# Turning the rows of the ternary weight by DMA instead of by TensorE, in a gated attention and feed-forward kernel

## The chip, the cores and the metric

The kernel runs on one core of a Trainium2 chip. The core has TensorE (PE, matrix products), VectorE (DVE), ScalarE (ACT), GpSimd (POOL) and SyncE (SP). SP and POOL mainly issue DMAs here, and the DMAs of all queues are carried by the core's 16 DMA engines. The metric is the device time of one execution in microseconds (us), the median of several.

## The reference

There are two batches of 1024 rows; a row has 2048 numbers. W is a 2048 x 2048 weight.

```python
def fake_quant(x, scale, zp):
    q = clip(round(x / scale + zp), 0, 255)
    return (q - zp) * scale

h   = x + tanh(g_xattn) * fake_quant(layernorm(x)) @ fake_quant(ctx)      # per batch: 1024x2048 @ 2048x2048

y   = layernorm(h)
s   = 127 / max(|y|) of each row
yq  = clip(round(y * s), -128, 127) / s
sw  = 1 / mean(|W|)
tw  = clip(round(W * sw), -1, 1)                                          # -1, 0 or 1
out = h + tanh(g_ffn) * (yq @ tw.T) / sw
```

The second product needs W's input index on the partitions (the axis that TensorE sums over), while W lies in memory with its output index first. So each block of 128 rows of W is rounded to bytes, limited to -1, 0 and 1, and turned.

## The kernel before

The function `centred` (line 344) runs when the zero points are 128. Rows are handled in tiles of 128, so a batch has 8 tiles (`MT`); `resid` holds the 8 tiles of the batch in work and is reused by the second one. An `arena` of 32 slots in SBUF holds everything large: loaded f32 rows (two slots each, `wide`), the quantized context (one slot for 256 of its rows and half of its columns), the turned activations (`aT` for the first product, `qT` for the second), and the turned W (`wt`, 8 slots, each with four row blocks and half of the input index, in float8). A pool named q8 (`bytes_`, `NB` = 4 buffers of 128x2048 bytes) holds a tile between its rounding and its turning. PSUM gives three accumulators `mm` and two small buffers `tr` for turning.

Bytes are turned as pairs: two neighbouring bytes are seen as one 16-bit value, TensorE transposes 128x128 of these against an identity matrix into `tr` (lines 494 and 1035), and the result holds pairs (j = 0, 1) side by side, which the later matmuls read with a stride. For the activations, two copies of 128x1024 from `tr` make f16 (line 502). For W, `weight_turn` (line 1021) does, for each of the 16 row blocks `ot`: `quant` on ACT (line 1028: f32 to rounded bytes, in a q8 buffer), `turn` on PE (eight transposes, line 1035), and `clip` twice (two halves of 1024 columns, from `tr` to float8 in a slot of the arena), on DVE as a max and min (line 1045) or on ACT as a sign (line 1043).

The work runs in these stages, which overlap: the first product of batch 0 (`first`, matmuls of line 622, in two halves h of the columns, evicted by DVE at line 628); loading W once for its mean (`weight_load`, line 977, `weight_sum`); `norm2`, which gives `qT` (lines 660, 666, 716); turning W, for which nine of the 16 blocks are loaded a second time; the second product of batch 0, in pairs of tiles with one quarter q of the output columns (`couple`, matmuls of line 759, q = 0 in single row blocks of W) and then tile by tile (`plain`, line 805), evicted by DVE at line 743 and stored by SP (line 750); meanwhile loads of batch 1's context (line 589) and rows (line 468) on POOL's queue; sums and differences of W's quarters on DVE (line 842), written to DRAM and brought back; then batch 1: first product (line 622) and the second one in seven products instead of eight (`seven`, line 930).

The order on each engine is fixed when the kernel is built. Every piece is a `step` of the planner `Order` (line 108), with an engine (or a choice of two, of which the planner takes the one that ends first), an estimated duration, a due time, what it reads and writes, the buffer that it takes and those that it gives back, and for DMAs the time that they hold the DMA engines. The planner lays all steps out twelve times, moves due times back from the end each time, and keeps the shortest layout. Each engine then works through its list in that order, and a step whose input is late holds up all those behind it on its engine.

Of the kernel before, what the change touches and what calls it, by code (L numbers as in the profile page):

```python
# [11 lines left out]
I16 = mybir.dt.int16  # L12
F8 = mybir.dt.float8e4
AF = mybir.ActivationFunctionType
ALU = mybir.AluOpType
# [8 lines left out]
class Plan:  # L24
# [9 lines left out]
    def step(self, engine, weight, due, do, rd=(), wr=(), take=None, give=(), dma=0.0, hold=0.0):  # L34
        n = len(self.steps)
        after = set()
        for key in rd:
            if key in self.writer:
                after.add(self.writer[key])
        for key in wr:  # L40
            after.update(self.readers.pop(key, ()))
            if key in self.writer:
                after.add(self.writer[key])
            self.writer[key] = n
        for key in rd:
            self.readers.setdefault(key, []).append(n)
        after.discard(n)
        self.steps.append((engine, weight, due, do, after, take, tuple(give), dma, hold))
        return n
# [58 lines left out]
class Order:  # L108
# [64 lines left out]
    def run(self, due):  # L173
        steps, N = self.steps, len(self.steps)
        waits = [len(s[3]) for s in steps]
        early = [s[7] for s in steps]
        pools = {k: [(0.0, -1)] * n for k, n in self.sizes.items()}
        left = dict(self.users)
        till = {}
        free, open_ = {}, {}  # L180
        dma_free, dma_last = 0.0, -1
        begin, end, where, slots = [0.0] * N, [0.0] * N, [None] * N, [None] * N
        pred = [[] for _ in steps]
        links = self.links = [{} for _ in steps]
        last = {}
        order = []

        def put(n):
            for e, w in steps[n][0]:
                open_.setdefault(e, {})[n] = w  # L190

        for n in range(N):
            if not waits[n]:
                put(n)
        for _ in range(N):
            best = None
            for e, cand in open_.items():
                fe = free.get(e, self.START.get(e, self.BRANCH))
                for n, w in cand.items():
                    at = early[n]  # L200
                    if at < fe:
                        at = fe
                    if best is not None and at > best[0] + 1e-6:
                        continue
                    take = steps[n][4]
                    if take:
                        at = max(at, self.room(pools[take[0]], *take[1:]))
                        if at == float("inf"):
                            continue
                    if len(steps[n][0]) > 1:  # L210
                        key = (at, due[n], n, at + w, e)
                    else:
                        key = (at, due[n], n, 0.0, e)
                    if best is None or at < best[0] - 1e-6 or key[1:] < best[1:]:
                        best = key
            if best is None:
                self.stuck = [n for c in open_.values() for n in c], order, slots
                return None
            at, _, n, _, e = best
            ways, _, _, _, take, give, dma, _ = steps[n]  # L220
            if len(ways) > 1:
                ends = []
                for e2, w2 in ways:
                    ends.append((max(at, free.get(e2, self.BRANCH)) + w2, e2, w2))
                fin, e, w = min(ends)
                at = fin - w
            else:
                w = ways[0][1]
            for e2, _ in ways:
                del open_[e2][n]  # L230
            if take:
                pool = pools[take[0]]
                idx = slots[n] = self.pick(pool, at, *take[1:])
                for i in idx:
                    if pool[i][1] >= 0:
                        pred[n].append(pool[i][1])
                        links[n][pool[i][1]] = True
                    pool[i] = (float("inf"), -1)
            if e in last:
                pred[n].append(last[e])  # L240
            last[e] = n
            begin[n] = at
            where[n] = e
            fin = at + w
            free[e] = fin
            if dma:
                if dma_last >= 0:
                    pred[n].append(~dma_last)
                dma_free = max(dma_free, fin) + abs(dma)
                dma_last = n  # L250
                fin = dma_free + self.LANDING
            end[n] = fin
            order.append(n)
            for m, i in give:
                for j in range(steps[m][4][1]) if i is None else (i,):
                    left[m, j] -= 1
                    t = till.get((m, j))
                    if t is None or fin + self.LAG > t[0]:
                        t = (fin + self.LAG, n)
                    till[m, j] = t  # L260
                    if not left[m, j]:
                        pools[steps[m][4][0]][slots[m][j]] = t
            for m in self.follow[n]:
                same = len(steps[m][0]) == 1 and steps[m][0][0][0] == e and not dma
                t = fin + (0.0 if same else self.LAG)
                if t > early[m]:
                    early[m] = t
                waits[m] -= 1
                if not waits[m]:
                    put(m)  # L270
        return order, begin, end, where, slots, pred
# [72 lines left out]
def centred(  # L344
# [15 lines left out]
    nc = tc.nc  # L360
# [5 lines left out]
    MT, OT = M // P, O // P  # L366
# [1 line left out]
    H, U = 1024, 512  # L368
    NQ = N // U
    I8 = mybir.dt.int8  # L370
    NS, NB = 32, 4
    SLOT = 2048

    const = ctx.enter_context(tc.tile_pool(name="const", bufs=1))
# [28 lines left out]
    def slot16(s):  # L403
        return arena[:, s * SLOT : (s + 1) * SLOT]
# [30 lines left out]

    Q_COST = {"PRE": 0.5, "SP": 0.5, "POOL": 0.7}
    turned = {}

    def parameters():
        s = {}  # L440
# [32 lines left out]
    def rsqrt(v, sd):  # L473
# [7 lines left out]
        nc.vector.scalar_tensor_tensor(r, e, 1.5, r0, ALU.add, ALU.mult)  # L481
        return r

    def turn_steps(t, key, q, q_by, due, name, pieces=1):

        s = {}

        def turn(i, slots=None):
            if slots is not None:
                s["pt"] = tr[slots[0]]  # L490
            pt = s["pt"].bitcast(F16).rearrange("p (c r) -> p c r", c=C)
            v = q["q"].bitcast(F16)
            for c in range(i * C // pieces, (i + 1) * C // pieces):
                nc.tensor.transpose(pt[:, c, :], v[:, ts(c, P)], ident)  # L494

        def spread(h, engine, slots=None):
            if h == 0:
                turned[name, t] = slots[0]
            d = slot16(turned[name, t]).rearrange("p (c j m) -> p c j m", c=C, j=2)
            v = s["pt"].bitcast(I8).rearrange("p (c m j) -> p c j m", c=C, j=2)  # L500
            n = C // 2
            (nc.scalar.copy if engine == "ACT" else nc.vector.tensor_copy)(  # L502
                d[:, ts(h, n)], v[:, ts(h, n)]
            )

        by = None
        for i in range(pieces):
            n = step(
                "PE", 0.05 + 0.55 / pieces, due - 50, (lambda i: lambda slots=None: turn(i, slots))(i),
                rd=[key("q", i)], wr=[key("pt", i)], take=None if i else ("tr", 1),  # L510
                give=[q_by] if i == pieces - 1 else [],
            )
            by = by if i else n
        ways = (("ACT", 1.1), ("DVE", 1.3))
        first_ = step(
            ways, 0, due - 20, lambda e, slots: spread(0, e, slots), rd=[key("pt", 0)], wr=[(name, t, 0)],
            take=("ar", 1, 0, home_t), give=[by],
        )
        step(
            ways, 0, due - 20, lambda e: spread(1, e), rd=[key("pt", pieces - 1), (name, t, 0)],  # L520
            wr=[(name, t, 1)], give=[by],
        )
        turned[name, t, "by"] = first_
# [357 lines left out]
    def seven(ta, tb, due, final=False):  # L881
# [22 lines left out]
        qa, qb = ([("qT", t, i) for i in range(2)] for t in (ta, tb))  # L904
        by = step("DVE", 0.7, due - 3, lambda slots: sums(0, slots), rd=qb, wr=[("S", ta, 1)], take=("ar", 2, 0, pairs_d))
        step("DVE", 0.7, due - 3, lambda: sums(1), rd=qa[:1], wr=qb[:1] + [("S", ta, 3)])
        step("DVE", 0.7, due - 3, lambda: sums(2), rd=qa[:1] + [("S", ta, 1)], wr=[("S", ta, 2)])
        step("DVE", 0.7, due - 3, lambda: sums(3), rd=qa[1:] + [("S", ta, 2)], wr=[("S", ta, 4)])
        products = (
            ("P1", "A", lambda: half(ta, 0), (0, 0), qa[:1], True, (ta, 0)),  # L910
            ("P2", "C", lambda: half(ta, 1), (0, 1), qa[1:], True, (ta, 0)),
# [109 lines left out]
    def weight_turn(ot, due):  # L1021
# [15 lines left out]
        def clip(h, engine, slots=None):  # L1037
# [10 lines left out]
            "ACT", 2.1, due, quant, rd=[("wl", ot), ("sw",)], wr=[key("q")], take=("q8", 1),  # L1048
            give=[wl[ot]["by"]],
        )  # L1050
        p = step("PE", 0.6, due - 50, turn, rd=[key("q")], wr=[key("pt")], take=("tr", 1), give=[by])
        for h in range(2):
            need = [key("pt")] + ([("w", q, 0, h)] if o else [])
# [946 lines left out]
```

## Time and profile before

| | |
|---|---|
| time, median of 3 runs | 492.32 us (491.85 to 495.02) |
| time of the profiled execution | 494.64 us |
| its span | 492.9 us |
| PE busy | 457.8 us, 93% of the span |
| DVE busy | 335.1 us, 68% |
| ACT busy | 262.8 us, 53% |
| transposes of W on PE, line 1035 | 128 instructions, 9.6 us busy |
| limiting of W on DVE, line 1045 | 23 instructions, 27.3 us |
| limiting of W on ACT, line 1043 | 9 instructions, 9.1 us |
| rounding of W on ACT, line 1028 | 16 instructions, 31.3 us |
| moved by DMA | 102.20 MB, mean 207 GB/s |

The span runs from the first to the last instruction that the profiler recorded; the time of an execution includes a little around it (1.74 us here). Busy time of matmuls overlaps at their ends, since they are pipelined: eight transposes in a row show 0.61 us of busy time, though the next matmul starts 0.45 us after the first of them. "PEld" is the loading of weights into TensorE, beside the matmuls.

### The profile page before, as it was taken

Reading aid. Unit: us, or ns where it says so; the run is one execution under the profiler, and the core shown is the slowest. Engines: PE = TensorE matmul, PEld = TensorE weight load, DVE = VectorE, ACT = ScalarE, POOL = GpSimd, SP = SyncE. Lnnn points to the kernel's source line nnn. Section 1 sums busy time; section 2 is a strip of 40 time slices with the busy share of each in tenths; the row PEclk is TensorE's granted clock in tenths of the full one; section 3 lists DMA queues with packets and bytes.
Section 4 is the critical chain, followed back from the end, with each engine's and each line's share of the span. In section 5 each row is a group of like instructions: output and inputs, shape, how many; then the busy total and the mean of one; then the engine's idle time right before and its main releaser. Section 6 shows DMA issues by size and latency. Waiting matters only on the chain.

```text
span 492.9 us, 6309 instructions
## 1 busy us (share of the span) xinstructions
PE 457.8 (93%) x2564; PEld 225.6 (46%) x2564; DVE 335.1 (68%) x522; ACT 262.8 (53%) x203; POOL 21.7 (4%) x39
## 2 busy tenths in 40 slices
PE   0489999999999898999998989999999999999995
PEld 0134444445576654444444435444444444444442
DVE  4778973588599897769997877223578887343432
ACT  3678987687799988831117678101366853000000
POOL 0000000000002120021011100000000000000000
PEclk9999999999999999999999999999999999999999
DMA  6999988990445985399999750053000012231304
GB/s 208 397 423 421 421 319 332 420 429 41 172 172 231 367 302 211 91 343 391 422 345 325 257 215 1 1 179 163 1 0 1 1 43 88 85 128 44 128 8 169
DMA packets 21853, 102.20 MB, mean 207 GB/s; under 512 B 1976, under 2 KB 1976, under 8 KB 16696
## 3 DMA queue, kind: packets, MB, share of 16 engines
q1 hardware_dynamic: 15008, 67.11, 34.2%
q0 software_dynamic: 6800, 34.61, 19.6%
q8 instruction: 22, 0.36, 0.3%
q14 instruction: 15, 0.12, 0.1%
q10 hardware_dynamic: 8, 0.00, 0.0%
HBM read 80.74 MB, written 20.97 MB: 206 GB/s over the span
## 4 chain that ended last, share of the span: by engine, by line
PE 65%; DMA 14%; issue 12%; DVE 3%; ACT 3%; SPq 1%; POOL 1%; POOLq 0%; ACTq 0%
PE mm L622 41%; PE mm L930 20%; DMA arena<-in_ctx_dram 14%; PE tr L494 2%; ACT arena L593 1%; ACT bytes L567 1%; PE mm L805 1%; SPq L1961 1%; DVE strip L666 1%; POOL arena L589 1%; DVE arena L1045 1%; DVE arena L502 0%; DVE resid L743 0%; PE mm L759 0%; POOL arena L977 0%
## 5 line engine op out<-in xcount | busy, mean ns | idle before, releaser
L622 PE MATMUL mm<-arena 128*128 128x512 f16 x1024 | 229.8, 383 | 7.9 <-DVE arena L597 4.6
L622 PEld LDWEIGHTS <-arena 128*128 128x128 f16 x1024 | 99.6, 99 | 125.0 <-issue 9.3
L743 DVE SCALAR_TENSOR_TENSOR resid<-mm,am,resid 128x1024 f32<-128x1024 f32 (+1 forms) x53 | 58.1, 1097 | 59.7 <-PE mm L930 47.9
L930 PE MATMUL mm<-arena 128*128 128x512 fp8e4 x448 | 97.5, 379 | 0.0
L593 ACT ACTIVATE arena<-arena,scal 128x2048 int16<-128x2048 f32 x32 | 63.3, 1999 | 47.3 <-DMA arena<-in_ctx_dram 36.4
L628 DVE SCALAR_TENSOR_TENSOR resid<-mm,scal,resid 128x1024 f32<-128x1024 f32 x32 | 40.9, 1278 | 49.4 <-PE mm L622 38.1
L930 PEld LDWEIGHTS <-arena 128*128 128x128 f16 x448 | 43.7, 98 | 51.9
L759 PE MATMUL mm<-arena 128*128 128x128 fp8e4 (+1 forms) x448 | 58.5, 288 | 1.7 <-DVE resid L743 1.7
L805 PE MATMUL mm<-arena 128*128 128x512 fp8e4 x256 | 55.9, 379 | 0.0
L660 ACT ACTIVATE arena<-resid,strip 128x2048 f32<-128x2048 f32 x16 | 32.0, 1998 | 39.5 <-DVE strip L654 35.4
L502 ACT CAST arena<-tr 128x1024 f16<-128x1024 int8 x39 | 37.8, 1011 | 16.9 <-PE tr L494 7.5
L759 PEld LDWEIGHTS <-arena 128*128 128x128 f16 x448 | 33.4, 98 | 24.1 <-issue 2.0
L666 DVE TENSOR_REDUCE strip<-arena 128x1 f32<-128x2048 f32 x16 | 36.5, 2280 | 5.1 <-ACT arena L660 5.1
L531 DVE BATCH_NORM_STATS2 stats<-resid 128x6 f32<-128x512 f32 x64 | 39.7, 675 | 0.0
L805 PEld LDWEIGHTS <-arena 128*128 128x128 f16 x256 | 24.9, 98 | 29.5
L567 ACT ACTIVATE bytes<-resid,strip 128x2048 int8<-128x2048 f32 (+1 forms) x17 | 33.0, 1987 | 7.7 <-DVE strip L550 5.9
L716 ACT ACTIVATE bytes<-resid,strip 128x2048 int8<-128x2048 f32 x16 | 32.7, 2087 | 6.7 <-DVE strip L689 6.7
L842 DVE TENSOR_TENSOR arena<-arena 128x2048 fp8e4<-128x2048 fp8e4 x16 | 36.0, 2281 | 0.0
L502 DVE CAST arena<-tr 128x1024 f16<-128x1024 int8 x25 | 30.3, 1218 | 7.1 <-PE tr L494 6.8
L1028 ACT ACTIVATE bytes<-arena,scal 128x2048 int8<-128x2048 f32 x16 | 31.3, 1999 | 0.8 <-DVE scal L1014 0.8
L1045 DVE TENSOR_SCALAR arena<-tr 128x1024 fp8e4<-128x1024 int8 x23 | 27.3, 1216 | 6.1 <-PE tr L1035 6.1
L494 PE MATMUL tr<-ident,bytes 128*128 128x128 f16 x256 | 20.6, 225 | 11.5 <-ACT bytes L567 9.2
(59 smaller groups left out, 184.5 us busy)
## 6 DMA issues: line engine op xcount, KB each, us to landing
arena<-in_ctx_dram SPq DMA_DIRECT2D x16, 1024.0 KB, 15.4
arena<-in_L_ffn_weight_dram SPq DMA_DIRECT2D x16, 1024.0 KB, 12.6
arena<-in_ctx_dram POOLq DMA_DIRECT2D x16, 1024.0 KB, 8.7
out_dram<-resid SPq DMA_DIRECT2D x31, 512.0 KB, 4.7
arena<-in_L_ffn_weight_dram POOLq DMA_DIRECT2D x9, 1024.0 KB, 6.6
resid<-in_x_dram POOLq DMA_DIRECT2D x8, 1024.0 KB, 11.6
resid<-in_x_dram SPq DMA_DIRECT2D x7, 1024.0 KB, 14.7
awayT<-arena SPq DMA_DIRECT2D x8, 512.0 KB, 7.5
```

What stands on the lines that cost most here:

```text
L502: (nc.scalar.copy if engine == "ACT" else nc.vector.tensor_copy)(d[:, ts(h, n)], v[:, ts(h, n)])
L531: nc.vector.bn_stats(stats6[:, t % 4, c, :], res(t)[:, ts(c, 512)])
L567: nc.scalar.activation(q["q"][:, ts(g, w)], res(t)[:, ts(g, w)], AF.Identity, bias=s["bi"][:, i : i + 1], scale=s["sc"][:, i : i + 1],)
L593: nc.scalar.activation(slot16(slots[0]).bitcast(I16), s["w"], AF.Identity, scale=rs2)
L622: nc.tensor.matmul(pm[t][:, ts(q, U)], a[:, c, j, :], o[:, j, ts(q, U)], start=(c + j == 0), stop=(c + j == C),)
L628: nc.vector.scalar_tensor_tensor(v, pm[t], g1, v, ALU.mult, ALU.add, accum_out=acc[:, i : i + 1])
L666: nc.vector.tensor_reduce(s["vm"][:, n + i : n + i + 1], s["dev", t], AX.X, ALU.max)
L743: lambda: nc.vector.scalar_tensor_tensor(v, ps(), am2[:, t : t + 1], v, ALU.mult, ALU.add),
L759: nc.tensor.matmul(ps[:, o0 * P : o1 * P], a[:, c, j, :], w[:, j, o0:o1], start=(c + j == 0), stop=(c + j == C),)
L805: nc.tensor.matmul(s["pm"][:, ts(i, U)], a[:, c, j, :], w[:, j, :], start=(c + j == 0), stop=(c + j == C),)
L842: nc.vector.tensor_tensor(slot8(s[k, n])[:, w], slot8(at(a))[:, w], slot8(at(b))[:, w], op, saturate=False)
L930: nc.tensor.matmul(s[bank][:, ts(n, U)], a[:, c, j, :], v[:, c, j], start=new and c + j == 0, stop=c + j == 4, skip_group_check=not new,)
```

## The change

W's row blocks no longer go through TensorE and PSUM. After the rounding on ACT, a DVE instruction (`flat`) limits all 2048 bytes of each row in place in the q8 buffer, reading int8 and writing float8. Two DMAs on SP's queue then turn the block, each for half of it: the source is 128 rows of 512 pairs of bytes, seen as int16, and the destination is the place in the arena's slot where `clip` wrote before. The q8 buffer is given back by the two DMAs instead of by the transposes on PE, and there are five such buffers instead of four. The planner counts a turning DMA with its own time to landing. `turn_far` would do the same for activations, but `by_dma` names only blocks of W, so it is never called. In `seven`, two sums also count as readers that give back a slot of `qT`.

```diff
-                fin = dma_free + self.LANDING
+                fin = dma_free + self.LANDING if dma > 0 else fin - 2 * dma + self.LANDING
...
-    NS, NB = 32, 4
+    NS, NB = 32, 5
...
+    by_dma = {("w", ot) for ot in range(OT)}
...
     def turn_steps(t, key, q, q_by, due, name, pieces=1):
 
+        if (name, t) in by_dma:
+            return turn_far(t, key, q, q_by, due, name)
...
-        step("DVE", 0.7, due - 3, lambda: sums(2), rd=qa[:1] + [("S", ta, 1)], wr=[("S", ta, 2)])
-        step("DVE", 0.7, due - 3, lambda: sums(3), rd=qa[1:] + [("S", ta, 2)], wr=[("S", ta, 4)])
+        step("DVE", 0.7, due - 3, lambda: sums(2), rd=qa[:1] + [("S", ta, 1)], wr=[("S", ta, 2)], give=[turned["qT", ta, "by"]])
+        step("DVE", 0.7, due - 3, lambda: sums(3), rd=qa[1:] + [("S", ta, 2)], wr=[("S", ta, 4)], give=[turned["qT", ta, "by"]])
...
             "ACT", 2.1, due, quant, rd=[("wl", ot), ("sw",)], wr=[key("q")], take=("q8", 1),
             give=[wl[ot]["by"]],
         )
+        if ("w", ot) in by_dma:
+
+            def flat():
+                nc.vector.tensor_scalar(s["q"].bitcast(F8), s["q"], -1.0, 1.0, ALU.max, ALU.min, saturate=False)
+
+            def far_turn(h, slots=None):
+                if slots is not None:
+                    wt[q, h] = slots[0]
+                d = slot16(wt[q, h]).bitcast(I16)[:, ts(o, U)].rearrange("p (c m) -> p c m", c=4)
+                nc.sync.dma_start_transpose(d, s["q"].bitcast(I16)[:, ts(h, U)])
+
+            step("DVE", 1.3, due, flat, wr=[key("q")])
+            for h in range(2):
+                step(
+                    "SP", 0.8, due, (lambda h: lambda slots=None: far_turn(h, slots))(h),
+                    rd=[key("q")] + ([("w", q, 0, h)] if o else []), wr=[("w", q, o, h)],
+                    take=None if o else ("ar", 1, 0, home_w), give=[by], dma=-0.8,
+                )
+            return
         p = step("PE", 0.6, due - 50, turn, rd=[key("q")], wr=[key("pt")], take=("tr", 1), give=[by])
```

More of the change, by code (lines that the diff above doesn't have):

```diff
@@ L482, in rsqrt, with turn_far, turn, spread @@
         return r
+    def turn_far(t, key, q, q_by, due, name):
+        def turn(slots):
+            turned[name, t] = slots[0]
+            d = slot16(slots[0]).bitcast(I16)[:, H:].rearrange("p (c r) -> p c r", c=C)
+            nc.sync.dma_start_transpose(d, q["q"].bitcast(I16))
+        def spread(h, engine):
+            d = slot16(turned[name, t]).rearrange("p (c j m) -> p c j m", c=C, j=2)
+            v = slot16(turned[name, t])[:, H:].bitcast(I8).rearrange("p (c m j) -> p c j m", c=C, j=2)
+            n = C // 2
+            (nc.scalar.copy if engine == "ACT" else nc.vector.tensor_copy)(d[:, ts(h, n)], v[:, ts(h, n)])
+        n = turned[name, t, "by"] = step(
+            "SP", 1.1, due, turn, rd=[key("q", 0)], wr=[(name, t, 0), (name, t, 1)], take=("ar", 1, 0, home_t),
+            give=[q_by], dma=-1.4,
+        )
+        step((("ACT", 1.1), ("DVE", 0.75)), 0, due, lambda e: spread(0, e), wr=[(name, t, 0)])
+        step("ACT", 1.1, due, lambda: spread(1, "ACT"), rd=[(name, t, 0)], wr=[(name, t, 1)])
     def turn_steps(t, key, q, q_by, due, name, pieces=1):
+        if (name, t) in by_dma:
+            return turn_far(t, key, q, q_by, due, name)
         s = {}
@@ L1050, in weight_turn @@
         )
+        if ("w", ot) in by_dma:
[12 more added lines that the diff above has]
+                    take=None if o else ("ar", 1, 0, home_w), give=[by], dma=-0.8,
+                )
+            return
         p = step("PE", 0.6, due - 50, turn, rd=[key("q")], wr=[key("pt")], take=("tr", 1), give=[by])
```

## The prediction

> **What bounds the kernel now.** I read the strip of the page first: PE is at nine tenths or more almost everywhere from the third slice on. Then the stage that the change touches, from the first rounding of W (123.9 us) to the limiting of its last block (202), as one window (busy us of PE, weight loads, DVE, ACT, POOL, each with its instructions; then granted clock, DMA share, GB/s):
>
> ```profile
> PE   0489999999999898999998989999999999999995
> ...
> 124.00:202.00 78.00, 73.76 (x659) 46.31 (x658) 65.75 (x101) 71.49 (x51) 10.03 (x16) 1.00 0.66 243
> ```
>
> In these 78 us PE is busy for 73.8, ACT for 71.5 and DVE for 65.8: three engines are nearly full, and DMA has a third of its time free. What W's turning costs there is in the groups by line:
>
> ```profile
> L1045 DVE TENSOR_SCALAR arena<-tr 128x1024 fp8e4<-128x1024 int8 x23 | 27.3, 1216 | 6.1 <-PE tr L1035 6.1
> L1035 PE MATMUL tr<-ident,bytes 128*128 128x128 f16 x128 | 9.6, 219 | 1.5 <-DVE arena L502 1.5
> L1043 ACT ACTIVATE arena<-tr 128x1024 fp8e4<-128x1024 int8 x9 | 9.1, 1020 | 5.7 <-DVE arena L1045 4.5 <-PE tr L1035 1.2
> ```
>
> The timeline of PE shows what a block costs TensorE, and how late W comes (start, duration, instructions, idle time before in brackets):
>
> ```profile
> 194.35 0.61 PE L494 MATMUL tr<-ident,bytes 128*128 128x128 f16 x8
> 196.49 0.61 PE L1035 MATMUL tr<-ident,bytes 128*128 128x128 f16 x8 [1.52 <-DVE arena L502]
> 196.93 3.62 PE L759 MATMUL mm<-arena 128*128 128x512 fp8e4 x16
> 200.38 0.61 PE L1035 MATMUL tr<-ident,bytes 128*128 128x128 f16 x8
> 201.39 17.43 PE L759 MATMUL mm<-arena 128*128 128x512 fp8e4 x80 [0.39 <-DVE resid L743]
> ```
>
> From the transposes' start at 196.49 to the next matmul is 0.44 us; the chain that ended last gives a block 0.45. The last block is turned only 1 us before the products of the last quarter run on, so W is made just in time. Last, that chain leaves PE between 138 and 265 us and goes through DVE, POOL's queue and the loads of batch 1:
>
> ```profile
> 229.11 19.04 DMA arena<-in_ctx_dram
> ...
> 250.54 8.72 DMA arena<-in_ctx_dram
> ...
> 262.80 2.10 ACT bytes L567
> ...
> 264.94 0.62 PE tr L494 x8
> ```
>
> So PE sets the time, and batch 1's inputs are close behind: PE waits 1.24 us at 264.9 and 2.00 at 287.9, then runs without a gap to the last eviction.
>
> **The change, part by part.**
>
> *PE loses the transposes:* 16 blocks x 0.45 us = **-7.2 us**, all on the path.
>
> *PE's waits in this stage* are 0.50 + 0.48 + 1.34 + 1.52 + 0.39 = 4.2 us. The 0.48 (a transpose waiting for line 1043) and the 1.52 (for a buffer `tr` behind DVE's copies) come from the two `tr` buffers, which W no longer takes. **-2.0**; the others wait for evictions and I leave them.
>
> *DVE and ACT:* 23 x 1.216 = 28.0 us leave DVE and 9 x 1.02 = 9.2 leave ACT. DVE gets 16 `flat` of 128x2048, int8 to float8, both in SBUF. No row has this. The bounds are line 597 (one input, 16 bits, SBUF to SBUF, same size) with 0.684 us, and line 842 (float8, two inputs, same size) with 2.281. With two inputs, 16 bits take 0.686 us for 1024 columns (line 900) and 8 bits 2.281 for 2048, so 8 bits go at half the rate. Some 0.15 us of each is fixed (line 531: 0.675 for 512, line 666: 2.280 for 2048, so 1.045 ns per column and 0.14 left). Line 597 halved in rate is 0.15 + 2 x 0.534 = **1.22 us**, the value I take, as the operation and places are those of line 597. 16 x 1.22 = 19.5: DVE -8.5, ACT -9.2. With 2.281 it would be 36.5: DVE +8.5, ACT -9.2, so nothing for the two together. These gains are not on PE's path themselves; they let W arrive earlier, which PE needs once it is faster.
>
> The Trainium skill, "VectorE: DVE Perf Modes", section "The perf-mode tier table (the rule you actually need)", gives a fp32 scalar operation in SBUF twice the plain rate, 1227 ns for 2048, and has no column for bytes. By it a `flat` would be an estimated 1.23 us; the trace of before can't show it.
>
> *The turning DMAs:* 32 on SP's queue, 128 KB each, no transposing DMA in the trace. The issue costs SP 0.33 us by the stores, and SP issues nothing between about 100 and 175.8 us; behind it stand the stores of line 750, which let batch 1's rows in. Time to landing: 4.2 us for a store of 256 KB, 4.4 for 512 KB at the start, 15.4 in the median for 1024 KB in a crowd. How long a turning DMA holds up the next one is bounded by 128 KB at the 423 GB/s of the busiest slices, 0.31 us, and by a full landing of 4.2 us. I take 1 us held and 4 us to landing: 128 KB lies nearer to the first bound by its size, but a turned block is moved in finer pieces than a plain one, so I leave it three times the plain 0.31. That fills 32 us of the queue within 75, with room.
>
> The Trainium skill pulls both ways. "VectorE: DVE Perf Modes", section "The three transpose paths", puts a 128x128 transpose at 390 ns on TensorE and 1309 ns by DMA and advises TensorE where PSUM will do. If those followed one another, 128 tiles would take an estimated 168 us and W would be some 90 us late. "DMA: Bandwidth & Descriptors", section "Latency and other measured facts", has 261 GB/s for transposing DMAs: 4.19 MB in an estimated 16 us, no bound at all. The row against the first rule is that PE's eight transposes cost 0.45 us here, not 3.1; nothing in the trace decides for the DMA.
>
> *The way of a block gets longer:* after rounding it was 0.6 (PE) + 1.2 (limiting) = 1.8 us; now 1.22 + 4 = 5.2, so +3.4. For the early blocks PE has 20.3 us of line 622 in this stage to put first. For the last block it shows: ACT, relieved by up to 9.2 us, rounds it that much earlier, 3.4 go to the longer way, so W is done 5.8 us earlier, while PE wants it 9.2 earlier. Of these 3.4 I count **+2.3**, the rest goes into matmuls with blocks already there. A block now keeps its q8 buffer for 2.0 + 1.2 + 4 = 7.2 us; 16 blocks and 6 tiles of `qT` in 78 us are one in 3.5, so two or three of the five buffers are in use: no wait.
>
> *Planner, `seven`, `turn_far`:* a reader more and code that is never called cost nothing. A new layout reorders everything; that is worth plus or minus 3 us either way, about the sum of PE's gaps from 260 to 300 (3.2).
>
> **Sum:** -7.2 - 2.0 + 2.3 = -6.9 us. The profiled execution took 494.64 us (span 492.9), 2.3 above the median, and would become 487.7; set against the median, 492.3 - 7 = **485.3 us**.
>
> Does it reach the end? At 265 us PE would come 7 us earlier and batch 1 has to keep up. POOL's loads wait for slots that ACT's rounding frees (15.3 and 57.6 us in the waits) and its row loads for stores (14.4): these come earlier with ACT and PE. From 220 to 260 DMA is full at 374 to 400 GB/s, but from 190 to 220 it has half its time free, so the loads can move forward.
>
> **Rivals.**
>
> 1. *Batch 1 takes the gain back* (or `flat` runs at 2.28 us and W is no earlier). For it: the chain above with 14% of the span in the context's loads, and DVE, ACT and POOL each in fixed order. Against it: the free DMA time before 220 us. PE then waits 7 us more near 265; at most 2 us are kept: 490 to 493.
>
> 2. *The turning DMAs are the new bound: slower.* They follow one another on one queue. W's blocks start at about 127 us and the last is needed at about 201; 32 in 74 us is 2.3 us each. Above that PE waits in the last quarters of the `couple`s. At 2.8 us each: 32 x 0.5 = 16 us late, less 9 saved: about 499. At the 4.2 us bound: 61 late, over 540. For it: no row, the skill's slow figure, and the ring shared with POOL's loads, which fill it from 160 to 190 us. Against it: 0.31 us of data.
>
> 3. *The change does less than it says*: the DMAs move bytes in place as PE did, so only the PE time could fail to go; the matmul count must fall by 128, and I give this nothing of its own.
>
> **Chances.** Forecast (479 to 487.3): 0.58. Rival 1 or a wash (within 1%, 487.4 to 497.2, about what a measurement here can tell from no change): 0.18. Slower, rival 2: 0.24. The lower end, 478, has all PE gaps of 120 to 300 us gone too (7.2 + 4.2 + 3.2 = 14.6). Upwards the range takes in rival 1 and the first part of rival 2, up to 502; what is left out is the DMA above 2.9 us each.
>
> **What would show it.** No line 1035, PE 9 to 10 us less busy; 16 `flat` near 1.2 us; 32 turning DMAs landing in 3 to 5 us; no PE wait of more than 1 us on them; PE's gaps near 265 and 288 no larger than before; the last product's start at 7 us less. A PE that waits for SP's DMAs, SP stores that come late, or a larger wait at 265 would make it wrong.

## The result, and the profile after

The changed kernel takes 517.82 us in the median of four runs (513.51 to 521.07), the kernel before 492.14 on the same chip: a ratio of 1.0495 (95% interval 1.0443 to 1.0546). It is 5% slower, where 1.4% faster was forecast, and outside the range (478 to 502). An execution more than 1.5% above the fastest of its kernel counts as slow here, and the ratios leave it out. The profiled execution took 513.51 us with a span of 511.7, against 494.64 and 492.9 before.

The page of the changed kernel, PE's busy share and granted clock in 40 slices, and the stage of W's turning as the same window as before (busy us of PE, weight loads, DVE, ACT, POOL, granted clock, DMA share, GB/s):

```profile
PE   0488999999859239989999999999999999999995
...
PEclk9999999999959759999999999999999999999999
...
124.00:202.00 78.00, 51.94 (x429) 33.49 (x427) 43.24 (x70) 44.90 (x32) 12.20 (x14) 0.80 0.74 203
```

There is a hole in PE between the tenth and the sixteenth slice, and in the same 78 us ACT and DVE have lost 27 and 23 us as well: none of the three is the bound there, all wait. The granted clock fell with PE's idling, to 0.80 over this window. The groups that answer to those of W's turning before:

```profile
L1078 DVE TENSOR_SCALAR bytes<-bytes 128x2048 fp8e4<-128x2048 int8 x16 | 19.3, 1225 | 3.7 <-ACT bytes L1052 3.7
L740 ACT ACTIVATE bytes<-resid,strip 128x2048 int8<-128x2048 f32 x16 | 33.0, 2089 | 35.2 <-DMA arena<-bytes 35.2
L783 PE MATMUL mm<-arena 128*128 128x128 fp8e4 (+1 forms) x448 | 61.3, 300 | 10.9 <-DMA arena<-bytes 9.1
```

The limiting (line 1078) costs what was expected, 1.225 us. But ACT's rounding of the activations (line 740 here, 716 before) waits 35.2 us for the turning DMAs, which hold the q8 buffers, and PE waits for them itself. The timeline of PE shows where (start, duration, instructions, idle time before in brackets):

```profile
146.27 1.01 PE L783 MATMUL mm<-arena 128*128 128x128 fp8e4 x8 [8.09 <-DMA arena<-bytes]
...
186.09 1.03 PE L518 MATMUL tr<-ident,bytes 128*128 128x128 f16 x8 [16.92 <-ACT bytes L740]
...
189.88 5.24 PE L783 MATMUL mm<-arena 128*128 128x512 fp8e4 x16 [1.05 <-DMA arena<-bytes]
...
225.84 17.43 PE L783 MATMUL mm<-arena 128*128 128x512 fp8e4 x80 [1.76 <-DVE resid L767]
```

Four waits, 27.8 us, against 4.2 in this stage before; the two later ones of before (3.2 us, at 265 and 288) are gone. So PE idles about 20.4 us longer. By the two profiles, the part of the span in which PE is not busy went from 35.1 to 55.7 us, 20.6 more. Without the transposes PE's busy time should have fallen by 16 x 0.45 = 7.2 us (their own 9.6 us counts the overlap with the next matmuls) and fell by 1.8 (457.8 to 456.0): eight small matmuls that take 0.61 us at full clock took 1.01 after the wait. I put the 5.4 us between down to the lower clock. -7.2 + 5.4 + 20.6 = 18.8, the difference of the spans.

The chain that ended last goes through single turning DMAs (start, duration, what):

```profile
130.75 15.49 DMA arena<-bytes
...
161.69 22.18 DMA arena<-bytes
...
202.03 11.20 DMA arena<-bytes
```

Half a row block, 128 KB, took 15 and 22 us here. For the line that issues them the trace gives the issues on SP (durations in ns, minimum, median, maximum) and the landings of all 32:

```profile
L1084 SPq DMA_TRANSPOSE arena<-bytes x32: 1190/1291/9112, 129.3 to 218.1; - x32
...
DMA to landing us min/median/max: 2.3/5.7/25.9
```

### The profile page after: what moved, and what is told of

Read it like the earlier page. It is cut to its first block, busy times and chain, and to the rows that moved or that the text cites. A ratio compares the mean times of both kernels' runs of the same rounds, so it can differ in the third digit from the quotient of the medians.

```text
span 511.7 us, 6110 instructions
## 1 busy us (share of the span) xinstructions
PE 456.0 (89%) x2436; PEld 222.2 (43%) x2436; DVE 329.2 (64%) x517; ACT 253.4 (50%) x193; POOL 25.0 (5%) x39
## 3 DMA queue, kind: packets, MB, share of 16 engines
q0 software_dynamic: 6800, 34.61, 19.3%
## 4 chain that ended last, share of the span: by engine, by line
PE 72%; DMA 16%; ACT 4%; DVE 3%; issue 2%; SPq 2%; ACTq 0%
PE mm L646 37%; PE mm L954 19%; DMA arena<-bytes 10%; PE mm L829 9%; PE mm L783 4%; DMA resid<-in_x_dram 4%; PE tr L518 2%; ACT arena L617 2%; DMA arena<-in_ctx_dram 2%; DVE strip L690 1%; SPq L2004 1%; DVE resid L767 1%; SPq L1084 1%; DVE arena L526 0%; DVE bytes L1078 0%
## 5 line engine op out<-in xcount | busy, mean ns | idle before, releaser
L646 PEld LDWEIGHTS <-arena 128*128 128x128 f16 x1024 | 100.3, 99 | 126.1 <-issue 11.0
L783 PE MATMUL mm<-arena 128*128 128x128 fp8e4 (+1 forms) x448 | 61.3, 300 | 10.9 <-DMA arena<-bytes 9.1
L954 PEld LDWEIGHTS <-arena 128*128 128x128 f16 x448 | 43.6, 98 | 51.5
L829 PE MATMUL mm<-arena 128*128 128x512 fp8e4 x256 | 55.7, 379 | 0.0
L526 DVE CAST arena<-tr 128x1024 f16<-128x1024 int8 x28 | 34.0, 1218 | 33.1 <-PE tr L518 31.3
L783 PEld LDWEIGHTS <-arena 128*128 128x128 f16 x448 | 35.6, 103 | 34.8 <-issue 12.2
L740 ACT ACTIVATE bytes<-resid,strip 128x2048 int8<-128x2048 f32 x16 | 33.0, 2089 | 35.2 <-DMA arena<-bytes 35.2
L526 ACT CAST arena<-tr 128x1024 f16<-128x1024 int8 x36 | 35.3, 1008 | 25.2 <-PE tr L518 22.5
L518 PE MATMUL tr<-ident,bytes 128*128 128x128 f16 x256 | 21.8, 233 | 26.2 <-ACT bytes L740 16.9
L829 PEld LDWEIGHTS <-arena 128*128 128x128 f16 x256 | 25.0, 98 | 30.0
L518 PEld LDWEIGHTS <-bytes 128*128 128x128 f16 x256 | 18.4, 105 | 34.4 <-ACT bytes L740 17.1
## 6 DMA issues: line engine op xcount, KB each, us to landing
arena<-in_L_ffn_weight_dram SPq DMA_DIRECT2D x16, 1024.0 KB, 11.5
```

Source lines behind the costliest of these rows:

```text
L646: nc.tensor.matmul(pm[t][:, ts(q, U)], a[:, c, j, :], o[:, j, ts(q, U)], start=(c + j == 0), stop=(c + j == C),)
L783: nc.tensor.matmul(ps[:, o0 * P : o1 * P], a[:, c, j, :], w[:, j, o0:o1], start=(c + j == 0), stop=(c + j == C),)
L829: nc.tensor.matmul(s["pm"][:, ts(i, U)], a[:, c, j, :], w[:, j, :], start=(c + j == 0), stop=(c + j == C),)
L954: nc.tensor.matmul(s[bank][:, ts(n, U)], a[:, c, j, :], v[:, c, j], start=new and c + j == 0, stop=c + j == 4, skip_group_check=not new,)
```

## What the queues carry

The trace has every DMA packet. A turning DMA moves 256-byte packets on SP's queue (q1); POOL's second loads of W move 8 KB packets, its context loads 4 KB (q0). Three windows of the changed kernel, each with the packets, MB and share of the 16 DMA engines of a queue: 136 to 143 us (loads of W beside it), 180 to 184 (loads of context beside it), 196 to 199 (nothing beside it):

```profile
q0 software_dynamic: 397, 2.86, 97.4%
q1 hardware_dynamic: 397, 0.10, 6.4%
...
q0 software_dynamic: 370, 1.45, 92.2%
q1 hardware_dynamic: 370, 0.09, 11.3%
...
q1 hardware_dynamic: 1499, 0.37, 54.2%
```

397 to 397, and 370 to 370: in these windows, where both queues have work all the time, they take turns packet by packet, whatever a packet's size. (48 of the first 397 on POOL's queue are of 4 bytes, the others of 8 KB.) Beside W's loads of 8 KB the turning DMAs move 57 packets per us, beside the context's of 4 KB 92, alone 500. A half block has 512 packets, so it needs about 9 us beside W's loads and 1 us alone. That became theory 1. Theory 2 was that turning DMAs are too slow in themselves, theory 3 that the order, which the planner laid out for a landing of 3.6 us, was the loss.

## The experiments

Times are medians, unless two are given; ratios are to runs of the kernel before on the same chip (492.47 to 492.75 us in the median).

**Small second loads of W.**

```diff
-            queue(name).dma_start(out=s["w"], in_=weight[ts(ot, P), :])
+            n = K if name == "SP" else K // 16
+            queue(name).dma_start(out=s["w"][:, 0:n], in_=weight[ts(ot, P), 0:n])
```

> The changed kernel in the same order, but each of POOL's nine second loads of W brings 128 columns instead of 2048 (64 KB for 1 MB; the rest of W is left out, so W's values are not the right ones). Theory 1 (a turning DMA gives one packet of 256 bytes for each packet of up to 8 KB that POOL's loads have in flight): the wait of 8 us near 138 us goes, the one near 169 us shrinks, since three context loads still run there; 495 to 506 us. Theory 2 (the turning DMAs are too slow by themselves: about 1.25 us of SP's time each and one after another): nothing changes, 512 us or more. Theory 3 (the order was laid out for a landing of 3.6 us): as theory 1, since landings come near to that.

492.08 us, ratio 0.9987 (0.9966 to 1.0008): 26 us less than the changed kernel with the same order, and 3 us below the range that theory 1 gave. The landings fell to 3.8 us in the median and 11.2 at most. One long wait was left, where the context loads run:

```profile
167.53 6.43 PE L783 MATMUL mm<-arena 128*128 128x512 fp8e4 x16 [7.01 <-DMA arena<-bytes]
```

**Small second loads of W and small loads of the context.** The same for line 613, with 64 columns of 1024 on POOL's queue.

> As the run with small second loads of W, and POOL's loads of batch 1's context bring 64 of 1024 columns too (the rest of the context of batch 1 is left out). Theory 1: no plain packet is in the turning DMAs' way, they land in 2.5 to 4 us, PE has no wait on them above 1 us, and the saved transposes show: 478 to 488 us. Theory 2: still 505 us or more, with PE waiting for SP. Theory 3: as theory 1.

480.99 us in the median of two runs, ratio 0.9749 (0.9669 to 0.9830). PE's waits from 120 to 300 us are down to two evictions:

```profile
159.69 4.51 PE L784 MATMUL mm<-arena 128*128 128x128 fp8e4 x32 [1.31 <-DVE resid L768]
193.56 17.43 PE L784 MATMUL mm<-arena 128*128 128x512 fp8e4 x80 [0.40 <-DVE resid L768]
```

With 32 turning DMAs of the same size, issued by SP in the same way (landing in 3.1 us in the median and 4.0 at most), theory 2 falls. The order is the same, so the loads beside them are the cause. The 11.5 us below the kernel before are no price of the transposes alone: the kernel before was not run with loads that small, and lighter loads may help it too. Theories 1 and 3 agree so far: without the loads, the landings are near the planner's.

**Finer pieces of the loads on POOL's queue.**

```diff
+            n = 1 if name == "SP" else 4
+            for i in range(n):
+                queue(name).dma_start(out=s["w"][:, ts(i, K // n)], in_=weight[ts(ot, P), ts(i, K // n)])
```

> The changed kernel in the same order and with all its work, but each of POOL's loads is cut by columns so that a row's piece is 2 KB: the second loads of W into four DMAs, those of batch 1's context into two. Theory 1: the turning DMAs still give packet for packet, but a plain packet is a quarter or a half as long, so a turning DMA lands in some 4 to 6 us under load instead of 12 to 26, and the time falls to 490 to 500 us, POOL's longer issuing included. If the DMA engines were shared by bytes instead, or the sum of the bytes were the limit, the landings would not change: 512 us or more. Theory 2: 512 us or more.

513.68 and 527.65 us: a miss, in the range that the expectation gave to a sharing by bytes and to theory 2. From 129 to 200 us POOL's queue moved 3502 packets for 11.72 MB, so 3.3 KB each in the mean and not 2, against 2112 for 12.58 MB (6.0 KB) in the changed kernel:

```profile
q0 software_dynamic: 3502, 11.72, 69.6%
q1 hardware_dynamic: 8695, 2.10, 45.9%
```

Packets did get smaller, but only by half, and POOL now waited for its own earlier loads between issues, so plain loads were under way for longer: the turning DMAs landed in 11.6 us in the median. The run didn't test what it was made for, a packet of 2 KB beside the turning DMAs, and its time can't part the theories. Its packets do speak against a sharing by bytes: from 140 to 142 us, where POOL's queue takes 99% of the DMA engines, 191 of its packets (148 of 4 KB, the others of 4 bytes) stand beside 186 of SP's, so 93 turning packets per us go out, where it was 57 beside 8 KB.

**The true price in the order.**

```diff
-                fin = dma_free + self.LANDING if dma > 0 else fin - 2 * dma + self.LANDING
+                fin = dma_free + self.LANDING if dma > 0 else fin + 12.0
```

> The changed kernel, but the planner is told that a turning DMA lands 12 us after its issue instead of 3.6. Theory 3 (the wrong price in the order is the loss): the order puts other work first, PE's waits on the turning DMAs go, 492 us or less. Theory 1: the DMAs that meet POOL's loads need that long however they are ordered, five q8 buffers of about 16 us each carry one block in 3.2 us at best, so the quantizing waits for buffers; 498 to 512 us. Theory 2: 505 us or more.

497.19 and 505.42 us. The order matters much: told of a landing 12 us after the issue, the planner makes a kernel that gets back 20.6 us of the 25.7 us lost in the better of its two runs, with the loads still on POOL's queue. It lies between the ranges of theories 3 and 1, and 4.7 us above the kernel before. In the profiled run, the 505.42, the landings are still long, and PE waits 11.1 us for them in three places (total, times, longest):

```profile
PE mm L783 <- DMA arena<-bytes: 11.1, 3, 6.5
...
DMA to landing us min/median/max: 3.0/8.5/23.2
```

So theory 3 is a large part of the lost time, though not of the long landings: a late half block costs most where the order doesn't expect it. On one run, how large stays open.

**Only the last four, or only the first four blocks by DMA.**

```diff
-    by_dma = {("w", ot) for ot in range(OT)}
+    by_dma = {("w", ot) for ot in range(12, OT)}
```

The other run has `range(4)` there. From here on, either of a pair's two means in `norm2` may come first.

> Only the last four row blocks of W are turned by DMA, the other twelve by TensorE as before. Theory 1: these come when POOL's second loads of W are over and only context loads of 4 KB rows are left beside them, so they land in 4 to 10 us; four blocks less are 1.8 us less on PE, given back in part: 488 to 495 us. Theory 3 (the order alone): the same. If any turning DMA costs its PE time several times over, 496 us or more.

> Only the first four row blocks of W are turned by DMA. Theory 1: these meet POOL's second loads of W with rows of 8 KB, so PE waits for the first quarter's pieces near 138 to 146 us as in the changed kernel, some 5 to 9 us, and gets 1.8 us back: 495 to 503 us, more than with the last four. If the load beside them didn't matter, the two would agree.

Last four: 503.38 to 515.67 us, ratio 1.0257 (1.0146 to 1.0368), slower. First four: 492.74 us, ratio 0.9998 (0.9968 to 1.0028). Both expectations missed, and in opposite directions. Eight turning DMAs each; those of the last four blocks:

```profile
L1084 SPq DMA_TRANSPOSE arena<-bytes x8: 1406/3436/9942, 180.8 to 211.6; - x8
  PE mm L783: 16.0, 1
DMA to landing us min/median/max: 10.4/16.0/21.1
```

The size of the plain packets was not what counted most. Near 200 us the DMA engines are full (a share of 1.11 in the window from 180 to 222): seven context loads of 4 KB rows go out on POOL's queue, and SP's own queue has four stores of 512 KB beside the eight turning DMAs, so which of the two made a half block need 16 us isn't parted here. And these are the last blocks, for which PE has nothing left to do: one wait of 15.98 us. The first four landed in 7.9 us in the median, since only three second loads of W went out in their time (share 0.75 from 128 to 147), and PE still had matmuls of the first product to put before their readers; it waited 3.2 us. My reading, which no further run tests: what decides is how long plain transfers are queued beside a turning DMA, and how much other work its reader has.

**The change without a turning DMA** (`by_dma = set()`).

> The change with no block turned by DMA: five q8 buffers, the planner's line, and the two readers more in the sums remain. All theories: the same as before within 1% (489 to 496 us). If the fifth buffer or the new order were part of the loss, 500 us or more.

494.0 us, ratio 1.0023 (0.9985 to 1.0061). The fifth buffer, the planner's line and the two readers cost nothing that can be measured.

**All these loads on SP's queue, behind and before the turning DMAs.** The planner counts a turning DMA as one in line.

```diff
-                fin = dma_free + self.LANDING if dma > 0 else fin - 2 * dma + self.LANDING
+                fin = dma_free + self.LANDING
...
-                    "SP", 0.8, due, (lambda h: lambda slots=None: far_turn(h, slots))(h),
+                    "SP", 1.3, due, (lambda h: lambda slots=None: far_turn(h, slots))(h),
...
-            weight_load(ot, due - 8.0, "POOL", reserve=4, hold=scale_at - 10.0)
+            weight_load(ot, due - 8.0, "SP", reserve=4, hold=scale_at - 10.0)
...
-            context(1, h, c, s1 - 80.0 + 35.0 * h + 4.0 * c, "POOL", hold=s1 - 92.0 + 35.0 * h + 4.0 * c, reserve=5)
+            context(1, h, c, s1 - 80.0 + 35.0 * h + 4.0 * c, "SP", hold=s1 - 92.0 + 35.0 * h + 4.0 * c, reserve=5)
```

> The changed kernel with all its work, but W's second loads and batch 1's context loads go out on SP's queue, where the turning DMAs are, instead of POOL's; the planner counts a turning DMA as one in that line (1.3 us of SP, landing after what is ahead of it). Theory 1 (two queues share the DMA engines packet for packet, and small packets lose): in one queue a turning DMA waits for the loads issued before it, 2.5 us each, and then moves at its own pace, so landings are 3 to 8 us and the long ones (12 to 26 us) go; 484 to 496 us. If the turning DMAs only lacked bandwidth, whatever the queue, landings stay as they are and the time is 505 us or more.

487.53 us, ratio 0.9886 (0.9807 to 0.9964). The same with the third sum's reader added:

```diff
-        step("DVE", 0.7, due - 3, lambda: sums(1), rd=qa[:1], wr=qb[:1] + [("S", ta, 3)])
+        step("DVE", 0.7, due - 3, lambda: sums(1), rd=qa[:1], wr=qb[:1] + [("S", ta, 3)], give=[turned["qT", ta, "by"]])
```

> The run with W's second loads and batch 1's context loads on SP's queue again, in a layout where the third of the sums that read a slot of qT counts as a reader too (in that run and in those with the first or last four blocks, one slot was reused before this sum had read it, so one tile's values came from other data; the amount of work was the same). Theory 1 (two queues share the DMA engines packet for packet): as there, 484 to 490 us, faster than before by about 1%, turning DMAs landing in 3 us in the median.

487.50 us in the median of six runs, ratio **0.9876 (0.9845 to 0.9907)**: faster than before by 1.2%, clear of the noise though small, with all the work, and 30 us faster than the changed kernel. The turning DMAs and PE's waits of that run, 120 to 300 us:

```profile
L1084 SPq DMA_TRANSPOSE arena<-bytes x32: 1189/1265/5117, 123.3 to 203.2; - x32
...
DMA to landing us min/median/max: 2.4/3.1/11.7
```

```profile
158.12 3.36 PE L783 MATMUL mm<-arena 128*128 128x128 fp8e4 x32 [3.18 <-DMA arena<-bytes]
168.31 7.07 PE L829 MATMUL mm<-arena 128*128 128x512 fp8e4 x32 [0.48 <-DVE resid L767]
223.91 8.40 PE L783 MATMUL mm<-arena 128*128 128x512 fp8e4 x32 [2.75 <-DVE resid L767]
```

**The control: the same prices, all loads on POOL's queue.** The same edits, without the two that move the loads.

> The control for the queue: all loads on POOL's queue as in the changed kernel, but the planner's prices as in the run with one queue (1.3 us of SP, landing behind the loads under way). Theory 1: the gain came from the queue, so this one still waits for turning DMAs that land in 8 us or more beside the loads: 498 to 515 us. Theory 3 (the order was the loss): 484 to 492 us, as with one queue.

516.11 us, ratio 1.0492 (1.0450 to 1.0534), as slow as the changed kernel and 1 us above theory 1's range; the landings' median is below the 8 us expected, their longest far above. Two waits of PE make most of it, and again the buffers:

```profile
155.88 1.04 PE L518 MATMUL tr<-ident,bytes 128*128 128x128 f16 x8 [12.46 <-ACT bytes L740]
171.93 3.79 PE L783 MATMUL mm<-arena 128*128 128x128 fp8e4 x32 [10.37 <-DMA arena<-bytes]
...
DMA to landing us min/median/max: 2.6/6.6/32.8
```

The bytes, the sizes, the number of transfers and the prices are those of the run before it, the layouts differ as the planner has another queue to fill. 29 us lie between them, and they belong to the queue together with its layout: on POOL's queue another order made 497.19 us (above), on SP's another one makes 499.17 (below), so the time alone does not part the two queues. The longest landing does: 11.7 to 12.1 us in the three runs that have these loads on SP's queue, 18.8 to 32.8 in the four that turn all of W beside the full loads on POOL's. Nor was room what was short: from 124 to 206 us the run with one queue moved 257 GB/s, the control 225 from 124 to 236.

Taking turns isn't the whole of it either. From 138 to 158 us of the control, 372 packets of POOL's queue and 1305 of SP's went out, only 151 GB/s with a DMA share of 1.18, where the changed kernel moved 424 GB/s from 136 to 143 with 1.04. So packets took longer there than in the windows above; why stays open.

**The kernel before with these loads on SP's queue**, W turned by TensorE.

> The kernel before (W turned by TensorE), but with W's second loads and batch 1's context loads on SP's queue. If the gain of the one queue comes from TensorE's saved transposes, this one stays within 1% of before (489 to 496 us). If it comes from the loads going out on SP, 484 to 488 us.

497.61 us, ratio 1.0088 (1.0054 to 1.0122), 1.6 us above the first case. So the move of the loads is no gain in itself; on one queue the kernel with turning by DMA is 497.6 - 487.5 = 10 us faster, about the saved transposes and a little of the waits. The layouts differ here too, so the 10 us are no clean price.

**Batch 1's rows on SP's queue too.**

> As the run before it, with batch 1's rows loaded on SP's queue as well, so that POOL issues no DMA. Theory 1: these loads start after the turning is over, so nothing is to be gained there: the same within 1% (483 to 492 us). If the loads of two queues hinder each other in general, 2 us or more faster.

499.17 us, ratio 1.0122 (1.0085 to 1.0159): a miss by 7 us and more. The layout changed as a whole, the loads stand before more of the turning DMAs (8.2 us to landing in the median, 11.9 at most), and PE's waits are spread over nine places. One queue bounds the long landings; it does not make the order good. Why the planner found no better layout here was not followed up.

## Why the prediction was wrong

- *What bounds the kernel now:* right. PE sets the time and W is made just in time; that is why late W costs so much.
- *PE loses the transposes, -7.2 us:* right in kind. The instructions are gone, and on one queue the whole change is worth 5.2 us against before, 10 against its own control. The sign "PE 9 to 10 us less busy" doesn't fit this term: it takes the 9.6 us that count the overlaps, where the sum has 7.2.
- *PE's waits for `tr`, -2.0:* those at 144.7 and 196.5 us are gone; the four of the changed kernel are 27.8 us.
- *DVE and ACT:* right: 1.22 us for `flat` was worked out from the halved rate of 8 bits, 1.225 measured; 19.3 us for the sixteen.
- *The turning DMAs, "1 us held and 4 us to landing":* **this is the step that failed.** With nothing beside them they behave so: issued 1.25 us apart, landing in 2.3 to 2.5 us. Over all 32 it is 5.7 us in the median and up to 25.9, the longest beside POOL's loads, and 2.8 us from one to the next. Both bounds came from plain DMAs, 0.31 and 4.2 us; I named the ring that is shared with POOL's loads only as a point for rival 2, gave it no price, and read DMA's free third as room. It was no question of room: the run with one queue moved 257 GB/s in this stage, the changed kernel 203. Where both queues were full, one packet of 256 bytes went out for one of 4 or 8 KB, and the order was laid out for a landing that didn't come.
- *The longer way of a block, +2.3, and "no wait" for q8 buffers:* both rest on the 4 us. With landings of up to 25.9 us the blocks kept the five buffers; ACT waited 35.2 us, and PE 16.9 us behind it. Mis-sized by the same term.
- *Planner, `seven`, `turn_far` at nothing:* right (1.0023), but a new layout can uncover a reader that was not counted.
- *Rival 1* did not come to bear: PE's waits at 265 and 288 us are gone, as PE came late.
- *Rival 2*, given 0.24, has the right sign, and its mechanism only in part. 32 DMAs took from 129.3 us to the end of the last issue at 219.7, 2.8 us each, for which it had 499 us; but the run with one queue spread its 32 over 123.3 to 203.2 us, 2.5 each, and lost nothing, so the rate of the queue was not the bound: single late half blocks were. Rival 2 left out that blocks late in the middle stop ACT and PE through the buffers, and that an idle PE gets a lower clock, 5.4 us here.

What the Trainium skill says on DMA can now be placed. The figure of 1309 ns for a transposed 128x128 in "VectorE: DVE Perf Modes", section "The three transpose paths", is not what a row of them costs: four such tiles were issued every 1.25 us where nothing was beside them. The advice for TensorE, quoted with it in the prediction, stands in that page's section "Rules for kernel authors". The 261 GB/s of "DMA: Bandwidth & Descriptors", section "Latency and other measured facts", given there for a middle dimension that is not contiguous, were not reached in the mean: 0.37 MB in 3 us are 123 GB/s, with the queue busy for 54% of the time. That was not the limit that counted.

## What to carry to other kernels

Be wary of a DMA of small packets beside bulk loads on another queue: put both on one queue, in an order that you choose, or keep them apart in time. One queue took the longest landings away in all three runs here and gained time in two of them, so the order has to be measured as well. Before moving work from an engine to DMA, look at what else is on the DMA engines in that very stage and in what packets; the free third of DMA said nothing here about how long one small transfer takes. And price a late buffer by all who wait for one: here PE's longest wait, 16.9 us, was for activations that ACT could not round for want of a buffer.

## What the runs showed of the hardware

- Where two queues were full they shared the DMA engines packet for packet: 397 to 397 beside packets of 8 KB, 370 to 370 beside 4 KB. Turning packets of 256 bytes moved at 57 and 92 per us there and at 500 alone.
- The issue of a turning DMA holds SP for 1.2 to 1.3 us alone and up to 9.1 us beside POOL's loads (from 171.4 us on), so all behind it on SP wait as well.
- A max and min from int8 to float8, 128x2048 in SBUF and in place, takes 1.225 us, against 0.684 for the 16-bit form and 2.281 for two float8 inputs: half and twice their rate, if some 0.15 us of each are fixed as the prediction works out.
- In its two long waits PE was granted the full clock for about 3.5 us and half of it after that: idle from 138.2 us, 1.00 up to 141 and 0.50 from 142 on; idle from 169.2, 1.00 up to 172 and 0.50 from 173 on. Eight small matmuls then took 1.01 us instead of 0.61. The full clock came back 6 to 7 us after the work did (work from 146.3 and 186.1 us, 1.00 again from 152.5 and 194).
